# A Mamba block with adaptive layer norm on one core: chunk products by row halves, one PSUM tile for each burst of them, one ring of six PSUM banks, and a reordered front part

## The chip, the cores and the metric

The kernel runs on one core of one Trainium2 chip. The metric is the device time of one execution in microseconds (us); lower is better. The kernel before takes 829.81 us, the median of three runs (829.78, 829.81 and 830.87 us). One further execution was recorded by the hardware profiler.

The engines are named as in the profile. PE is TensorE, and its weight loads are listed apart as PEld. DVE is VectorE, ACT is ScalarE, POOL is GpSimd, and SP issues the DMAs (SPq is its queue). PSUM is the memory that PE writes its results into; a "bank" is the unit in which the kernel's PSUM pool hands it out.

## The reference, cut to what matters

All data are float32. There are 4 sequences of 512 tokens with 512 features. A modulation vector is computed for each sequence, then comes a Mamba layer, and then a square feed-forward layer whose weights are reduced to signs times a row mean:

```python
mod = (silu(c) @ wmod).reshape(4, 6, 1, 512)          # sa, ca, ga, sb, cb, gb
h = layernorm(x) * (1 + ca) + sa
x = x + ga * mamba(h)                                 # ga, gb: kept away from 0 by 0.25
h = layernorm(x) * (1 + cb) + sb
x = x + gb * (h @ binarize(W).T + bias)

# mamba(h), with d_inner 1024, 8 groups of state 64, 64 heads of size 16, chunks of 128 tokens
x, B, C, z, A = split(h @ in_proj.T)                  # 1024, 512, 512, 1024, 64
x, B, C = silu(causal_conv4([x, B, C]) + bias)
dt = softplus(A);  A_cum = cumsum(-dt) inside a chunk
Y_diag = sum over s' <= s of  (C_s . B_s') * exp(A_cum_s - A_cum_s') * x_s'
state  = state * exp(sum of -dt in the chunk) + sum over s of  B_s * exp(A_cum_end - A_cum_s) * x_s
Y_off  = (C_s . state before the chunk) * exp(A_cum_s)
y = Y_diag + Y_off + D * x / dt
out = (y * silu(z + z_bias)) @ out_proj.T
```

The change touches the two products with C: the scores `C . B` inside a chunk and `C . state` across chunks. Both contract over the 64 state entries of one group.

## The kernel before, in words

**Tiling.** The 2048 tokens are cut into eight halves `h` of 256 tokens (two for each sequence), each half into two chunks `c` of 128. The eight groups are taken in four pairs `gp`, so that one pair fills 128 partitions: 64 state entries of group r = 0, then 64 of r = 1. A unit is one `(h, c, gp)`, and there are 64 units. Features lie on partitions during the projections and the convolution.

**Front part of a half.** `f_norm` and `f_hT` normalize and transpose the tokens. `f_dt` (L296) makes softplus, the cumulative sums `pc`, the totals `pe`, turned copies `pn` and `pr`, and stores sums, exponentials and reciprocals to DRAM (L347, L350, L362). `conv_pair` (L369) projects two tiles of 128 channels on PE (four accumulating products each, L367), scales on ACT (L379), adds three convolution taps on DVE straight from PSUM (L383), and ends with a tanh on ACT and a product on DVE (L391). It is called for B, C and x. For C the last product is written twice, into the two diagonal blocks of a tile `cd` that is zero elsewhere (three such tiles, cleared once, L112 to L116). `to_tokens` (L394) transposes B and x back to tokens-on-partitions through PSUM. `f_xt` (L424) also loads the reciprocals from DRAM (`rr`, one buffer) and multiplies on POOL (L442), which is the last use of the tile `u` of that convolution (tag "u", two buffers). `f_z` (L445) makes the gate.

**Units.** `stage0` loads the cumulative sums, spread over partitions, into two of four `decay` tiles, and the factors `e` (L480 to L493). `stage1` (L500) forms the scores `pg` for both groups in one product: stationary 128x128 from B, moving 128x256 from the zero-padded `cd` (L509). DVE masks them (L511), ACT takes 16 exponentials (L516), DVE multiplies (L519). `stage2` (L524) forms `C . state` in the same way into half of the tile `py` (L543, left out for the first chunk of a sequence), then the products with x: sixteen of 32 output columns each for the two groups, four of them side by side in the array (L549). DVE and POOL combine (L557 to L562), and the new state is made on PE (`pst`, L574, 64 output columns each).

**Tail of a chunk.** `tail1` to `tail3` (L601 to L638) do the output projection `po`, the second layer norm, and the feed-forward `pf`.

**PSUM.** Four banks with the tag "mm" (projections, `phT`, `po`, `ph`, `pf`), two with "tr" (transposes, the small products of `f_dt`, `pst`), one for `pg`, one for `py`.

**Order.** `FRONT` gives each front function a step relative to its half; `at` collects functions by step, and the loop at L676 issues them step by step, with one unit per step: `stage1` of the next unit, the functions of the step, `stage2` of this unit, `stage0` of the unit after next. That is the order of priority. [...]

Of the kernel before, what the change touches and what calls it, by code (L numbers as in the profile page):

```python
# [1 line left out]

# [13 lines left out]
P = 128  # L16
# [5 lines left out]
KS = 4  # L22
# [16 lines left out]
def adaln_mamba_block(  # L39
# [28 lines left out]
    ps = ctx.enter_context(tc.tile_pool(name="ps", bufs=4, space=PSUM))  # L68
# [42 lines left out]

    cds = []  # L112
    for i in range(3):
        cd = keep.tile([P, 2, 2, T], F32, name=f"cd{i}")
        nc.gpsimd.memset(cd, 0.0)
        cds.append(cd)  # L116
# [66 lines left out]
    def mod_cols(t6, slot):  # L183

        pg = mod_row(t6)
        row = wk.tile([B, DM], F32, tag="h2", name=f"row{t6}")
        nc.vector.tensor_scalar(row, pg, 1.0 if t6 in (1, 4) else 0.0, None, ALU.add)
        pm = ps.tile([P, NK, B], F32, tag="tr", bufs=2, name=f"pm{t6}")
        for dt in range(NK):
            nc.tensor.transpose(pm[:, dt, :], row[:, dt * P : (dt + 1) * P], ident[:B, :B])  # L190
        nc.vector.tensor_copy(modT[:, slot], pm)
# [12 lines left out]
    def gates_out():  # L204

        grow = wk.tile([B, 3, DM], F32, tag="gates", name="grow", bufs=1)
        brow = wk.tile([B, DM], F32, tag="th", name="brow", bufs=1)
# [88 lines left out]
    def f_dt(h):  # L296
# [6 lines left out]
        pa = ps.tile([P, W], F32, tag="tr", bufs=2, name=f"pa_{h}")  # L303
# [4 lines left out]
        u, r, s, q, acc, relu = (small(n) for n in ("du", "dr", "ds", "dq", "da", "dl"))  # L308
# [5 lines left out]
        nc.vector.tensor_mul(s, u, r)  # L314
        nc.vector.tensor_mul(q, s, s)
        nc.vector.tensor_scalar(acc, q, SERIES[0], None, ALU.mult)
        for cf in SERIES[1:]:
            nc.vector.scalar_tensor_tensor(acc, acc, cf, q, ALU.add, ALU.mult)
        nc.vector.scalar_tensor_tensor(acc, acc, 1.0, s, ALU.add, ALU.mult)
        nc.vector.scalar_tensor_tensor(acc, acc, 2.0, relu, ALU.mult, ALU.add)  # L320
        ndt = small("ndt", 2)
        nc.vector.tensor_scalar(ndt, acc, -1.0, None, ALU.mult)
        drdt = small("drdt")
        nc.vector.reciprocal(r, acc)
        nc.vector.tensor_mul(
            drdt.rearrange("p (c h) -> p c h", c=2), r.rearrange("p (c h) -> p c h", c=2), bc_mid(dsk, 2)
        )

        pe = ps.tile([P, 2, W], F32, tag="tr", bufs=2, name=f"pe_{h}")
# [12 lines left out]
        pc = ps.tile([NH, 2, 2, CH], F32, tag="tr", bufs=2, name=f"pc_{h}")  # L342
# [8 lines left out]
        pn = ps.tile([P, W], F32, tag="tr", bufs=2, name=f"pn_{h}")  # L351
        for c in range(2):
            nc.tensor.transpose(pn[:, c * NH : (c + 1) * NH], sh[:, c, :], ident[:NH, :NH])
        st = small("st", 2)
        nc.vector.tensor_scalar(st, pn, -1.0, None, ALU.mult)

        pr = ps.tile([NH, 2, CH], F32, tag="tr", bufs=2, name=f"pr_{h}")
# [5 lines left out]
        H[h].update(ed=ed, dec=dec, st=st)  # L363

    def proj(pm, h, col, lo):
        for k in range(NK):
            mm(pm, win[:, k, col : col + P], H[h]["hT"][:, k, lo:], start=(k == 0), stop=(k == NK - 1))  # L367

    def conv_pair(h, t0, name, dst=None):  # L369
# [4 lines left out]
        u = wk.tile([P, 2, T], F32, tag="u", name=f"u_{name}_{h}", bufs=2)  # L374
        for j in range(2):
            t = t0 + j
            pm = ps.tile([P, KS - 1 + T], F32, tag="mm", name=f"pp_{name}{j}_{h}")
            proj(pm, h, t * P, 0)
# [7 lines left out]
        th = wk.tile([P, 2, T], F32, tag="th", name=f"th_{name}_{h}", bufs=1)  # L386
        nc.scalar.activation(th, u, AF.Tanh)
        if dst is None:
            dst = [(u, slice(0, P))]
        for d, r in dst:  # L390
            nc.vector.scalar_tensor_tensor(d, th[r], 1.0, u[r], ALU.add, ALU.mult)  # L391
        return u

    def to_tokens(src, name):  # L394

        pt = ps.tile([P, 2, 2, P], F32, tag="tr", bufs=2, name=f"pt_{name}")
# [5 lines left out]
    def f_B(h, q):  # L402
        t = wk.tile([P, 2, T], F32, tag="B", name=f"B_{h}_{q}", bufs=3)
        conv_pair(h, DI // P + 2 * q, f"B{q}", [(t, slice(0, P))])
        H[h]["B"][q] = t

    def f_C(h, q):
        cd = cds[(2 * h + q) % 3]
        conv_pair(
            h, (DI + NG * NS) // P + 2 * q, f"C{q}",  # L410
            [(cd[r * NS : (r + 1) * NS, :, r, :], slice(r * NS, (r + 1) * NS)) for r in range(2)],
        )
        H[h]["C"][q] = cd
# [7 lines left out]
    def f_x(h, j):  # L421
        H[h]["xc"] = conv_pair(h, 2 * j, f"x{j}")

    def f_xt(h, j):  # L424
        xc = H[h].pop("xc")
# [8 lines left out]
        rr = wk.tile([P, 2, T], F32, tag="rr", name=f"rr_{h}_{j}", bufs=1)  # L434
# [10 lines left out]
    def f_z(h, j):  # L445
        pm = ps.tile([P, 2, T], F32, tag="mm", name=f"pp_z{j}_{h}")
        for q in range(2):
            proj(pm[:, q, :], h, NCONV + (2 * j + q) * P, KS - 1)
        u = wk.tile([P, 2, T], F32, tag="u", name=f"uz_{h}_{j}", bufs=2)
# [4 lines left out]
        th = wk.tile([P, 2, T], F32, tag="th", name=f"thz_{h}_{j}", bufs=1)  # L454
# [9 lines left out]
    U0, U1 = {}, {}  # L464
# [32 lines left out]
    def c_pair(h, c, gp):  # L497
        return H[h]["C"][gp // 2][:, gp % 2, :, c * CH : (c + 1) * CH]

    def stage1(h, c, gp):  # L500
# [7 lines left out]
        pg = ps.tile([P, 2, CH], F32, tag="g", name=f"pg_{n}", bufs=1)  # L508
        mm(pg, H[h]["B"][gp // 2][:, gp % 2, c * CH : (c + 1) * CH], c_pair(h, c, gp), start=True, stop=True)  # L509
        gm = wk.tile([P, 2, CH], F32, tag="gm", name=f"gm_{n}", bufs=3)  # L510
        nc.vector.tensor_mul(gm, pg, bc_mid(upto, 2))  # L511
# [12 lines left out]
    def stage2(h, c, gp):  # L524
# [16 lines left out]
        py = ps.tile([P, 2, 2, CH], F32, tag="y", name=f"py_{n}", bufs=1)  # L541
        if k > 0:
            mm(py[:, 1], states[b, k][:, gp, :], c_pair(h, c, gp), start=True, stop=True)  # L543

        for r in range(2):
            for q in range(2):
                for j in range(HPG // 2):
                    i = 2 * j + q
                    mm(py[32 * j : 32 * j + 32, 0, r, :], xp[:, r * 2 * P + 32 * i : r * 2 * P + 32 * i + 32],  # L549
                       ets[r][:, i, :], start=(q == 0), stop=(q == 1))  # L550
# [5 lines left out]
        if k > 0:  # L556
            nc.vector.tensor_mul(t, py[:, 1], e)  # L557
            nc.vector.tensor_add(t, py[:, 0], t)  # L558
            nc.gpsimd.tensor_add(t, t, xs)  # L559
        else:  # L560
            nc.vector.tensor_add(t, py[:, 0], xs)  # L561
        nc.gpsimd.tensor_mul(zg, t, zg)  # L562

        if k < HPB * 2 - 1:
# [6 lines left out]
            pst = ps.tile([P, P], F32, tag="tr", bufs=2, name=f"pst_{n}")  # L571
# [57 lines left out]
    def tail3(h, c):  # L629
# [9 lines left out]


    FRONT = [
        (1, load_x, ()), (2, f_norm, ()), (3, f_hT, ()), (3, f_dt, ()),
        (4, f_B, (0,)), (4, f_C, (0,)), (4, f_Bt, (0,)),
# [90 lines left out]
```

## Time and profile before

| | before |
|---|---|
| median of three runs | 829.81 us |
| profiled execution, its own time | 828.1 us |
| its span, first to last instruction | 826.4 us |
| granted TensorE clock, mean of the span | 0.98 |
| PE busy | 773.7 us, 94% |
| DVE busy | 647.4 us, 78% |
| ACT busy | 529.2 us, 64% |
| POOL busy | 258.2 us, 31% |
| DMA moved | 99.26 MB, 120 GB/s in the mean |

A float32 product shows in the profile as two MATMUL rows, so 64 products `pg` appear as x128. The time that the profile gives for one MATMUL runs to its modelled end; the pace of PE is read from one row's start to the next row's start. A form such as `128*64 128x128` reads: 128 rows and 64 columns of the array are used, and the moving operand is 128 partitions by 128 elements. In the list of groups, the numbers behind the bar are the busy time as a union, the mean duration of one, and the idle time of that engine just before.

### The profile page before, as it was taken

What the parts mean: (1) busy time and instruction counts of PE and PEld (TensorE: products, weight loads), DVE (VectorE), ACT (ScalarE), POOL (GpSimd) and SP (SyncE); (2) the same over time, 40 slices, a digit from 0 to 9 for tenths busy, and PEclk for the clock granted to TensorE, in tenths of its full rate; (3) what the DMA queues carried; (4) which work ended last, traced back from release to release, by engine and by line L of the source; (5) the groups of instructions that cost most, each with busy time, mean ns of one, the idle gap of its engine ahead of it and who ended that gap; (6) DMA issues with size and microseconds to landing.
All of it is one profiled execution on the core that took longest, in us unless ns stands there. A gap on an engine that the chain in (4) does not pass through costs nothing. (4 is left out here: it accounts for less than half of the span.)

```text
span 826.4 us, 14794 instructions
## 1 busy us (share of the span) xinstructions
PE 773.7 (94%) x5008; PEld 531.7 (64%) x5008; DVE 647.4 (78%) x1249; ACT 529.2 (64%) x1510; POOL 258.2 (31%) x293
## 2 busy tenths in 40 slices
PE   5979889999999999999999999999999999999875
PEld 0853657767667767667667767667667766667431
DVE  3688779995899669995899669996899768995742
ACT  0455485677667778577767678476758687676640
POOL 5020312353223412353223412253213521353431
PEclk9979999999999999999999999999999999999986
DMA  8856542525344372425444272344434382343620
GB/s 297 324 136 199 148 103 68 136 62 137 94 116 127 87 180 68 129 70 128 103 112 133 74 190 68 104 94 104 128 101 113 91 204 52 113 103 90 147 58 13
DMA packets 120139, 99.26 MB, mean 120 GB/s; under 512 B 73976, under 2 KB 98552, under 8 KB 120064
## 3 DMA queue, kind: packets, MB, share of 16 engines
q1 hardware_dynamic: 120064, 98.32, 44.9%
q8 instruction: 40, 0.66, 0.4%
q14 instruction: 35, 0.29, 0.1%
HBM read 92.50 MB, written 5.79 MB: 119 GB/s over the span
## 5 line engine op out<-in xcount | busy, mean ns | idle before, releaser
L516 ACT ACTIVATE decay<-decay,st 128x128 f32<-128x128 f32 x1024 | 313.8, 390 | 39.5 <-DMA decay<-sums_d 39.0
L519 DVE SCALAR_TENSOR_TENSOR decay<-decay,gm 128x1024 f32<-128x1024 f32 x128 | 168.4, 1322 | 11.4 <-ACT decay L516 10.6
L367 PE MATMUL pp_x<-hT,win 128*128 128x259 f32 x512 | 124.5, 393 | 3.4 <-DVE u_B L383 3.4
L606 PE MATMUL po<-wout,z 128*128 128x512 f32 x256 | 122.0, 615 | 5.3 <-POOL z L562 5.3
L367 PE MATMUL pp_z<-hT,win 128*128 128x256 f32 x512 | 115.1, 379 | 0.0
L367 PEld LDWEIGHTS pp_x<-hT,win 128*128 128x128 f32 x512 | 95.6, 193 | 23.0 <-issue 7.7
L367 PEld LDWEIGHTS pp_z<-hT,win 128*128 128x128 f32 x512 | 95.4, 189 | 15.7 <-issue 3.3
L549 PE MATMUL py<-decay,xpad 128*32 128x128 f32 x2048 | 81.8, 280 | 6.6 <-DVE decay L519 5.4
L383 DVE SCALAR_TENSOR_TENSOR u_x<-pp_x,cw,u_x 128x256 f32<-128x256 f32 x192 | 81.8, 476 | 2.2 <-ACT u_x L379 1.7
L442 POOL TENSOR_TENSOR xs<-u_x,rr 128x512 f32<-128x512 f32 x32 | 47.2, 1474 | 112.7 <-DVE u_x L391 68.1
L606 PEld LDWEIGHTS po<-wout,z 128*128 128x128 f32 x256 | 47.2, 194 | 51.6 <-issue 44.1
L549 PEld LDWEIGHTS py<-decay,xpad 128*32 128x32 f32 x2048 | 54.1, 111 | 36.0 <-issue 23.8
L569 POOL TENSOR_TENSOR xd<-xpad,ed 128x256 f32<-128x256 f32 x48 | 35.2, 732 | 131.4 <-PE pst L574 101.8
L562 POOL TENSOR_TENSOR z<-yt,z 128x256 f32<-128x256 f32 x64 | 66.7, 1042 | 30.4 <-DVE yt L561 18.9
L559 POOL TENSOR_TENSOR yt<-yt,xs 128x256 f32<-128x256 f32 x48 | 38.9, 811 | 111.1 <-DVE yt L558 110.9
L634 PE MATMUL pf<-bwT,h 128*128 128x512 f32 x128 | 63.5, 636 | 6.6 <-DVE u_x L383 5.8
L367 PE MATMUL pp_B<-hT,win 128*128 128x259 f32 x256 | 60.6, 382 | 0.0
L367 PE MATMUL pp_C<-hT,win 128*128 128x259 f32 x256 | 58.9, 381 | 0.0
L623 ACT ACTIVATE h<-ph,modT 128x128 f32<-128x128 f32 x64 | 24.5, 456 | 48.7 <-PE ph L621 48.7
L451 ACT ACTIVATE uz<-pp_z,zb 128x256 f32<-128x256 f32 x64 | 26.9, 466 | 43.7 <-PE pp_z L367 41.7
L367 PEld LDWEIGHTS pp_B<-hT,win 128*128 128x128 f32 x256 | 47.5, 190 | 11.2 <-issue 4.3
L367 PEld LDWEIGHTS pp_C<-hT,win 128*128 128x128 f32 x256 | 48.4, 190 | 7.4
(129 smaller groups left out, 1083.3 us busy)
## 6 DMA issues: line engine op xcount, KB each, us to landing
decay<-sums_d SPq DMA_DIRECT2D x128, 256.0 KB
decay<-sums_d SPq DMA_DIRECT2D x128, 128.0 KB
rr<-r_d SPq DMA_DIRECT2D x64, 128.0 KB
wm<-in_w_mod SPq DMA_DIRECT2D x24, 256.0 KB
e<-e_d SPq DMA_DIRECT2D x96, 64.0 KB
x<-in_x SPq DMA_DIRECT2D x16, 256.0 KB
win<-in_w_inT SPq DMA_DIRECT2D x4, 1024.0 KB
xr<-in_x SPq DMA_DIRECT2D x16, 256.0 KB
```

The lines of the kernel that those rows point to most:

```text
L367: mm(pm, win[:, k, col : col + P], H[h]["hT"][:, k, lo:], start=(k == 0), stop=(k == NK - 1))
L383: nc.vector.scalar_tensor_tensor(u[:, j, :], pm[:, k : k + T], cw[:, t, k : k + 1], u[:, j, :], ALU.mult, ALU.add)
L442: nc.gpsimd.tensor_tensor(xs, xc, rr, ALU.mult)
L451: nc.scalar.activation(u[:, q, :], pm[:, q, :], AF.Identity, bias=zb[:, 2 * j + q : 2 * j + q + 1], scale=0.5)
L516: nc.scalar.activation(ets[r][:, i, :], ets[r][:, i, :], AF.Exp, bias=H[h]["st"][:, hd : hd + 1])
L519: nc.vector.scalar_tensor_tensor(ets[r], ets[r], 1.0, bc_mid(gm[:, r, :], HPG), ALU.min, ALU.mult)
L549: mm(py[32 * j : 32 * j + 32, 0, r, :], xp[:, r * 2 * P + 32 * i : r * 2 * P + 32 * i + 32], ets[r][:, i, :], start=(q == 0), stop=(q == 1))
L559: nc.gpsimd.tensor_add(t, t, xs)
L562: nc.gpsimd.tensor_mul(zg, t, zg)
L569: nc.gpsimd.tensor_tensor(xd, xg, by_head(H[h]["ed"][:, hd0 : hd0 + HPP]), ALU.mult)
L606: mm(po, H[h]["z"][g // 2][:, g % 2, c * CH : (c + 1) * CH], wout[:, g, :], start=(g == 0), stop=(g == NKI - 1))
L634: mm(pf, h2[:, k, :], bwT[:, k, :], start=(k == 0), stop=(k == NK - 1))
```

## The change

In the words of the code:

- C is kept as one ordinary tile (tag "C", three buffers) with one closing product in `conv_pair`; the three zero-padded tiles are gone.
- Each product with C becomes two, one for each half of the partitions (64 rows of the array, 128 moving elements). The two halves write different halves of a new PSUM tile `gy`, 4 KB for each partition, one buffer. `burst(old, new)` makes the products with the state of unit `old` and the scores of unit `new`, two units ahead, into the same tile.
- `glued` puts every product of a burst, and every one of the eight products of a group's `py`, behind the first of them and at a priority 1000 places higher, so that they stand together in PE's queue.
- All other PSUM tiles, `py` among them, share the tag "mm" with six buffers.
- `f_dt` is cut into `f_dt`, `f_sums` and `f_turned_sums`. These two, `f_Bt` and `f_xt` are called through `behind`, which puts their PE instructions behind the last projection traced so far for that half, and `FRONT` places them one projection later than before.
- Buffers: "u" from two to four, "th" and "rr" from one to two, `ndt` from two to one; the tiles `ds` and `drdt` reuse `du` and `dr`.
- The tail functions of a step come behind the front functions of later halves. `stage0` and `stage1` of the unit two ahead follow `stage2` directly.

```diff
-    ps = ctx.enter_context(tc.tile_pool(name="ps", bufs=4, space=PSUM))
+    ps = ctx.enter_context(tc.tile_pool(name="ps", bufs=6, space=PSUM))
...
-    cds = []
-    for i in range(3):
-        cd = keep.tile([P, 2, 2, T], F32, name=f"cd{i}")
-        nc.gpsimd.memset(cd, 0.0)
-        cds.append(cd)
...
-        ndt = small("ndt", 2)
+        ndt = small("ndt")
...
+    def f_sums(h):
...
+    def f_turned_sums(h):
...
     def proj(pm, h, col, lo):
         for k in range(NK):
-            mm(pm, win[:, k, col : col + P], H[h]["hT"][:, k, lo:], start=(k == 0), stop=(k == NK - 1))
+            last = mm(pm, win[:, k, col : col + P], H[h]["hT"][:, k, lo:], start=(k == 0), stop=(k == NK - 1))
+        return last.ins
...
-        u = wk.tile([P, 2, T], F32, tag="u", name=f"u_{name}_{h}", bufs=2)
+        u = wk.tile([P, 2, T], F32, tag="u", name=f"u_{name}_{h}", bufs=4)
...
-        if dst is None:
-            dst = [(u, slice(0, P))]
-        for d, r in dst:
-            nc.vector.scalar_tensor_tensor(d, th[r], 1.0, u[r], ALU.add, ALU.mult)
+        nc.vector.scalar_tensor_tensor(u if dst is None else dst, th, 1.0, u, ALU.add, ALU.mult)
...
-        pt = ps.tile([P, 2, 2, P], F32, tag="tr", bufs=2, name=f"pt_{name}")
+        pt = ps.tile([P, 2, 2, P], F32, tag="mm", name=f"pt_{name}")
...
-        rr = wk.tile([P, 2, T], F32, tag="rr", name=f"rr_{h}_{j}", bufs=1)
+        rr = wk.tile([P, 2, T], F32, tag="rr", name=f"rr_{h}_{j}")
...
+    def glued(products):
+
+        first = products[0]()
+        with tc.issue_after(first.ins), tc.high_priority(offset=1000):
+            for product in products[1:]:
+                product()
+
+    def by_rows(gy, slot, h, c, gp, stationary):
+
+        return [
+            partial(
+                mm, gy[:, r, slot, :], stationary[part],
+                H[h]["C"][gp // 2][part, gp % 2, c * CH : (c + 1) * CH], start=True, stop=True,
+            )
+            for r, part in enumerate((slice(0, NS), slice(NS, P)))
+        ]
+
+    def burst(old, new):
+
+        gy = ps.tile([P, 2, 4, CH], F32, tag="gy", bufs=1, name="gy_" + "_".join(map(str, old or new)))
+        products = []
+        if old is not None:
+            h, c, gp = old
+            k = (h % HPB) * 2 + c
+            if k > 0:
+                products += by_rows(gy, 1, h, c, gp, states[h // HPB, k][:, gp, :])
+                G[old, 1] = gy
+        if new is not None:
+            h, c, gp = new
+            products += by_rows(gy, 0, h, c, gp, H[h]["B"][gp // 2][:, gp % 2, c * CH : (c + 1) * CH])
+            G[new, 0] = gy
+        glued(products)
...
-        pg = ps.tile([P, 2, CH], F32, tag="g", name=f"pg_{n}", bufs=1)
-        mm(pg, H[h]["B"][gp // 2][:, gp % 2, c * CH : (c + 1) * CH], c_pair(h, c, gp), start=True, stop=True)
...
-        py = ps.tile([P, 2, 2, CH], F32, tag="y", name=f"py_{n}", bufs=1)
-        if k > 0:
-            mm(py[:, 1], states[b, k][:, gp, :], c_pair(h, c, gp), start=True, stop=True)
+        py = ps.tile([P, 2, CH], F32, tag="mm", name=f"py_{n}")
...
+    def behind(h, f, *args):
+
+        with tc.issue_after(H[h]["last"]):
+            f(h, *args)
...
-        (4, f_B, (0,)), (4, f_C, (0,)), (4, f_Bt, (0,)),
-        (5, f_x, (0,)), (5, f_xt, (0,)), (5, f_x, (1,)), (6, f_xt, (1,)),
-        (6, f_B, (1,)), (6, f_C, (1,)), (6, f_Bt, (1,)),
-        (7, f_x, (2,)), (7, f_xt, (2,)), (7, f_x, (3,)), (8, f_xt, (3,)), (8, f_z, (0,)),
+        (4, f_B, (0,)), (4, f_C, (0,)), (5, f_x, (0,)), (5, behind, (f_sums,)), (5, behind, (f_Bt, 0)),
+        (5, f_x, (1,)), (5, behind, (f_turned_sums,)), (5, behind, (f_xt, 0)),
+        (6, f_B, (1,)), (6, f_C, (1,)), (6, behind, (f_xt, 1)),
+        (7, f_x, (2,)), (7, behind, (f_Bt, 1)), (7, f_x, (3,)), (7, behind, (f_xt, 2)),
+        (8, f_z, (0,)), (8, behind, (f_xt, 3)),
...
+        new = units[step + 2 : step + 3] if step >= 0 else units[0:2]
         if step < 0:
-            stage0(*units[0])
-        if 0 <= step < len(units):
+            for unit in new:
+                burst(None, unit)
+                stage0(*unit)
+                stage1(*unit)
+        elif step < len(units):
+            if new or not is_first(*units[step][:2]):
+                burst(units[step], new[0] if new else None)
             stage2(*units[step])
-        if ahead and late:
-            stage1(*units[step + 1])
-        if step + 2 < len(units):
-            stage0(*units[step + 2])
+            for unit in new:
+                stage0(*unit)
+                stage1(*unit)
```

## The prediction

> **What bounds the kernel now.** I read the page's busy lines and slices first, then the stretches by time, then the PE timeline, the waits, and last the groups.
>
> ```profile
> PE 773.7 (94%) x5008; PEld 531.7 (64%) x5008; DVE 647.4 (78%) x1249; ACT 529.2 (64%) x1510; POOL 258.2 (31%) x293
> PE   5979889999999999999999999999999999999875
> PEclk9979999999999999999999999999999999999986
> 192.00:284.00 92.00, 91.44 (x613) 65.17 (x612) 78.08 (x149) 65.43 (x188) 28.73 (x30) 1.00 0.45 111
> 284.00:376.00 92.00, 88.85 (x611) 62.67 (x610) 76.42 (x149) 64.20 (x184) 30.78 (x36) 1.00 0.44 107
> ```
>
> From 100 to 780 us PE is busy nearly throughout (91.4 and 88.9 of 92 us, one half each) at the full granted clock; DVE follows with 76 to 78 of 92. So what counts is PE time in each unit, and after that PE's few gaps. The timeline of PE for one stretch shows the units:
>
> ```profile
> 454.23 0.60 PE L509 MATMUL pg<-cd,B 128*128 128x256 f32 x2
> 454.66 3.60 PE L606 MATMUL po<-wout,z 128*128 128x512 f32 x8
> 458.09 0.60 PE L399 MATMUL pt_xt<-ident,u_x 128*128 128x128 f32 x4
> 458.53 7.08 PE L367 MATMUL pp_z<-hT,win 128*128 128x256 f32 x32
> 465.53 1.08 PE L549 MATMUL py<-decay,xpad 128*32 128x128 f32 x32
> 466.55 0.44 PE L574 MATMUL pst<-xd,bt 128*64 128x128 f32 x4
> 466.91 0.70 PE L509 MATMUL pg<-cd,B 128*128 128x256 f32 x2
> 467.45 0.60 PE L621 MATMUL ph<-ident,t 128*128 128x128 f32 x4
> ```
>
> Start to start, a `pg` among full-array products costs 454.66 - 454.23 = 0.43 us, and right behind `pst` 467.45 - 466.91 = 0.54. So the first product after a change of array shape pays some 0.10 more (its second weight load isn't covered). The change of shape itself: 32 `pp_z` rows at their pace of 0.216 are 6.91, but 7.00 passed until `py` started: 0.09 a change. Four 128-element transposes take 0.44, 0.11 a pass. `pst`, four passes in two column halves, takes 0.36 with the 0.09 on leaving, so 0.27: its halves run side by side.
>
> PE's waits, and two that stand behind them:
>
> ```profile
> PE pf L634 <- DVE u_x L383: 5.8, 3, 1.9
> PE pe L330 <- DVE ndt L322: 3.9, 4, 1.2
> PE pp_x L367 <- DVE u_B L383: 3.4, 2, 2.9
> PE pt_bt L399 <- DVE B L391: 1.8, 4, 0.7
> PE py L543 <- DVE yt L558: 1.2, 1, 1.2
> ACT u_B L379 <- POOL xs L442: 2.4, 1, 2.4
> POOL xs L442 <- DMA rr<-r_d: 38.7, 11, 11.7
> ```
>
> Some 58 us of PE gaps in the whole span (start-to-start beyond the pace above, slow clock after a gap included) lie at the start, at the end and in these places.
>
> **The change part by part.** Its own time is 828.1 us with a span of 826.4; the median is 829.8, so 1.7 us over the profiled execution, which I add at the end.
>
> *Products by row halves.* 64 `pg` and 48 `C . state` products, 112 in all, cost 0.43 each. Each becomes two products of 64 rows and 128 elements, four passes. No row of this profile runs two row halves at once. Run in turn, four passes cost 0.44 (the transposes' row): no gain. Run side by side, like `pst`, two rounds of 0.11: 0.22. I take 0.22, since `pst` is the nearest row: two halves of the array, the same number of passes and elements, different outputs. 112 x 0.21 = 23.5 us less; the other end is 0, and an extra cost is kept in the next term.
>
> That weight loads of different tiles can run together shows in this row of the groups:
>
> ```profile
> L549 PEld LDWEIGHTS py<-decay,xpad 128*32 128x32 f32 x2048 | 54.1, 111 | 36.0 <-issue 23.8 <-DVE decay L519 6.9 <-ACT decay L516 2.9
> ```
>
> 2048 loads of 111 ns are 227 us, done in 54.1. [...]
>
> *Shape changes.* There will be 66 bursts: two at the start, 62 with a new unit, two at the end with an old one alone. Each is a shape of its own. In front of `py` it adds one change (0.09) and its own uncovered second load (0.10): 66 x 0.197 = 13.0 more. The 0.10 that `pg` pays now is paid by the full-array product that follows. If other work always stands between burst and `py`, it is 0.197 more each, 26 in all. Glueing goes the other way: the PE timeline has 103 runs of `py` rows for 64 units (at 413.3 to 416.1 one unit's is cut into four by `pn`, `pr` and `pst`); I expect 80, so 23 x 2 x 0.093 = 4.3 less (0 to 7). Net +8.7, bounds +6 and +26.
>
> *Gaps.* Near 50 to 62 us PE sits 2.6 us before `py`, then 2.9 before `pp_x`, and runs some 2.3 us slower after that. There ACT waits for a `u` tile that POOL holds until `rr` has landed. Four `u` and two `rr` lift that; late next is DVE's convolution, so I count 5. `behind` puts a projection (3.5 us, 16 passes) ahead of `pe` and `pt_bt`, which takes their 3.9 + 1.8. For `pf <- u_x` (5.8, and 1.8 of slow clock at 520) a bank of "mm" is held by the taps; six banks against four help, but `py`, `pst` and transposes now compete for them: half, 3.8. Together 14.5; gaps here come back elsewhere, since DVE is at 84% in these stretches and its chains aren't shorter. I take 7 less; bounds 15 less and, if the shared ring is the tighter one (six "mm" with `py` among them against four, two and one before), 5 more.
>
> *DVE, ACT, POOL.* The two closing products of C (32 of 905 ns, 29.0 us busy) become 16 like the x ones (842 ns), 13.5: 15.5 us less on DVE, hidden under PE, worth 0; without that cover up to 15 less. The cleared `cd` tiles (2.7 us of POOL) lay beside the first weight loads: 0. Reused small tiles: no instruction fewer; `ndt` with one buffer must be read by `pe` and `pc` before the next half's, a half later: 0.
>
> *Queues.* `f_sums` moves its two stores on SP (0.64 and 0.55 at 413.5) behind the projections of B, C and x0, and `f_turned_sums` moves the store of `r_d` (0.87) behind x1's. Queued behind them on SP are the `decay`, `e` and `rr` loads; ACT's exponentials and POOL's `xs` wait for those. SP itself mostly waits (258 us for `py` to free a `decay` tile), and the next half's first unit is three steps away: 0 in the middle. At the start the sums are due at 37.9 us, with x's projections done at the same time: 0, at most 3.5 more. Tails behind fronts in a step only change what fills in: 0. `burst` ahead of `py` makes the next burst wait for the DVE readers of `gy`; the row of that kind is `py <- yt L558`, 1.2 us: 0, and a rival.
>
> Sum: -23.5 + 8.7 - 7 = -21.8. Profiled: 806.3; median 808.
>
> **The rivals.** *Row halves run in turn.* For it: nothing here shows rows side by side. Against: columns do, four at a time. Then 0 + 8.7 - 7 = +1.7: 831.5, between 824 and 840 with the other bounds.
>
> *The burst waits (slower).* `gy` has one buffer, so PE at a burst waits until DVE has read the previous one (mask and `yt`), and with old and new glued, for the later of two readers. If that leaves PE idle 0.6 us at each of 66 bursts, it adds 39.6: 848. It decides from 21.8 / 66 = 0.33 us. For it: at 454.2 the scores were ready and DVE masked them only at 457.1, 2.3 us after their end. Against: `pg` and `py` have one bank each now, and PE lost 1.2 us to that; projections fill in.
>
> *More than forecast.* Bursts always next to `py`, every gap named gone, some of the tail's too: -23.5 + 6 - 15 = -32.5, 797; with DVE's cover relieved as well, 788.
>
> **How the numbers follow.** Forecast (800 to 818): 0.48. More: 0.17. In turn: 0.18, of it 0.05 faster, 0.04 the same, 0.09 slower. Burst waits: 0.17, of it 0.02 faster, 0.15 slower. A difference of 0.2% (1.7 us) is about what the runs can tell, which spread by 1.1 us. Faster 0.48 + 0.17 + 0.05 + 0.02 = 0.72, same 0.04, slower 0.24. The range leaves out the worst of the waiting rival and the best of the gains: 788 to 838; the forecast's own is 800 to 818.
>
> **What would show it.** Right: the pace of a four-product burst near 0.54 (0.22 + 0.22 + 0.10) and not 0.9; about as many shape changes as before plus 40; `pe`, `pt_bt` and the start's `u_B` gone from PE's waits; the DVE busy time near 632. Wrong: first-pass rows of a burst 0.11 apart for r = 0 and 1 (in turn); a new wait of PE on the mask or `yt` at the head of the waits; idle PE beside a busy DVE in the middle; or a start longer than 100 us to the first unbroken stretch.

## The result and the profile after

The changed kernel takes 855.93 us (median of four runs, 847.62 to 858.37). The kernel before, run beside it on the same chip, takes 830.34 us (829.78 to 831.22). The ratio is 1.029 with a 95% interval of 1.022 to 1.036: slower, where 808.0 was forecast, and beyond the upper end of the range, 838. The profiled execution takes 855.14 us; its span is 853.4 us against 826.4 before. Runs of one kernel differ by up to 15 us here, with the clock that they are granted (0.960 in the fastest of the changed kernel's four, 0.945 in the slowest), so differences of a few us between two kernels say little.

The page's busy lines and slices of the changed kernel:

```profile
PE 775.4 (91%) x5232; PEld 537.0 (63%) x5232; DVE 613.4 (72%) x1233; ACT 521.3 (61%) x1510; POOL 240.2 (28%) x290
PE   4898799899989999999989999899989999999875
PEclk9999999999899999999999979999999989999967
```

PE is busy 91% of the span, not 94%, and there are 8s in the middle of its line where before had an unbroken row of 9s. The same two stretches as in the prediction (start and end, length, then busy time of PE, PEld, DVE, ACT and POOL, granted clock, DMA share, GB/s):

```profile
192.00:284.00 92.00, 87.47 (x630) 63.87 (x629) 70.58 (x143) 59.30 (x173) 25.91 (x29) 0.94 0.43 112
284.00:376.00 92.00, 87.35 (x628) 62.15 (x627) 71.64 (x144) 62.53 (x182) 28.80 (x37) 0.98 0.42 110
```

PE is idle 4.5 and 4.7 us in them, where it was idle 0.6 and 3.2 before. So no other engine became the bound: DVE's busy time fell too, from 78.1 and 76.4 us to 70.6 and 71.6. PE loses time to waits, and these are its waits (total us, times, longest):

```profile
PE pt_xt L401 <- DVE u_x L393: 23.8, 14, 3.4
PE pg L175 <- DMA wm<-in_w_mod: 10.9, 2, 7.9
PE py L498 <- DVE decay L546: 7.1, 5, 2.5
PE pa L301 <- ACT hT L285: 5.0, 6, 1.2
...
PE gy L498 <- DVE gm L538: 4.5, 3, 1.5
...
PE gy L498 <- DVE yt L585: 0.4, 1, 0.4
```

The first line is new. PE stands before the transposes of x until DVE has finished the convolution, 14 times. `pe <- ndt`, `pt_bt <- B` and `pp_x <- u_B`, which the change was to remove, are gone, and so is `pf <- u_x`. One of the 14 places in PE's timeline, with what stands around it (start, busy us, instructions, and in brackets the idle time before and its releaser):

```profile
433.04 0.66 PE L401 MATMUL pt_bt<-ident,B 128*128 128x128 f32 x4
433.54 3.67 PE L371 MATMUL pp_x<-hT,win 128*128 128x259 f32 x16
...
437.69 0.28 PE L357 MATMUL pn<-ident,sh 64*128 64x64 f32 x2
437.90 0.41 PE L363 MATMUL pr<-ident,dr 128*64 128x128 f32 x2
440.55 0.66 PE L401 MATMUL pt_xt<-ident,u_x 128*128 128x128 f32 x4 [2.24 <-DVE u_x L393]
441.04 0.60 PE L649 MATMUL ph<-ident,t 128*128 128x128 f32 x4
441.57 0.40 PE L498 MATMUL py<-decay,xpad 128*32 128x128 f32 x1
...
443.43 3.90 PE L371 MATMUL pp_B<-hT,win 128*128 128x259 f32 x13
```

`pp_B` at 443.43 needs `hT`, which `pp_x` had already used at 433.54, and a bank; that of `pt_bt` had been read out by ACT at 435.84. By these it could have filled the 2.24 us, but it ran behind `pt_xt`. It also shows a second loss behind this gap: 13 rows in 3.90 us are 0.30 each, where the pace is 0.216. The granted clock in short stretches from 438 to 447 us (PE busy, granted clock, DMA share, GB/s) goes with it:

```profile
438.00:441.00 3.00, 0.76 (x6) 1.00 0.18 43
441.00:443.00 2.00, 2.00 (x34) 0.66 0.00 1
443.00:445.00 2.00, 2.00 (x16) 0.50 0.45 144
445.00:447.00 2.00, 2.00 (x11) 0.99 0.67 200
```

**Where the 28.6 us between PE's first and last row went.** For each pair of PE rows I took the time from start to start beyond the pace of the row's own shape, and summed what exceeds 0.16 us. That is "gaps", slow clock included; the rest of the time from PE's first row to its last is "products and shapes". The gaps are split in two: time in which PE is idle (first to last row less the page's busy time), and busy time beyond products and shapes, for the most part, as I read it, rows stretched by a lower clock (the clock's record has 32.9 us of the span at half before and 84.1 in the changed kernel). Each row of the table is from one profiled execution; experiments 1 and 5 are below.

| | PE, first to last row | products and shapes | gaps | of them idle | of them stretched |
|---|---|---|---|---|---|
| before | 811.9 | 753.5 | 58.4 | 38.2 | 20.2 |
| changed | 840.5 | 737.1 | 103.4 | 65.1 | 38.3 |
| experiment 1 | 817.4 | 736.8 | 80.6 | 42.3 | 38.3 |
| experiment 5 | 805.4 | 735.7 | 69.7 | 45.1 | 24.6 |

So the part that the change was meant to save is saved, 16.4 us, and 45.0 us of new gaps cost more than that: 26.9 us of idle time and 18.1 us of stretched rows (the granted clock is 0.951 in the mean of the span, 0.980 before).

**The reason, by the order of PE's rows.** The order is that of the rows' start times. In the changed kernel 438 tiles take a buffer from the shared ring "mm", and their first writers run exactly in the order in which the program text asks for the tiles: none of the 438 is out of it. In the kernel before, of the 364 tiles in "mm" and "tr" (ten of the opening left out) none is out of order inside its own ring (224 and 140 tiles), but 97 are out of order across the two. So in these two profiles first writers left program order only from one ring to the other, never inside one. In the one ring no projection ran ahead of a transpose that the program asked for earlier, though the transpose still waited for DVE (23.8 us in 14 waits). The prediction's "projections fill in" was seen here only across rings.

### The profile page after: what moved, and what is told of

The parts are those of the page before. It is cut to its first block, busy times and chain, and to the rows that moved or that the text cites. A ratio compares the mean times of both kernels' runs of the same rounds, so it can differ in the third digit from the quotient of the medians.

```text
span 853.4 us, 15226 instructions
## 1 busy us (share of the span) xinstructions
PE 775.4 (91%) x5232; PEld 537.0 (63%) x5232; DVE 613.4 (72%) x1233; ACT 521.3 (61%) x1510; POOL 240.2 (28%) x290
## 4 chain that ended last, share of the span: by engine, by line
PE 71%; ACT 13%; DVE 8%; DMA 3%; issue 3%; POOL 1%; SPq 1%; DVEq 0%; ACTq 0%; POOLq 0%
PE po L634 12%; PE pp_z L371 12%; ACT decay L543 9%; PE pp_B L371 7%; PE pp_x L371 7%; PE pp_C L371 6%; PE pf L662 6%; PE py L501 4%; PE py L498 4%; DVE decay L546 3%; PE pa L301 3%; PE pt_xt L401 2%; PE pg L175 2%; PE pst L602 2%; PE gy L498 2%
## 5 line engine op out<-in xcount | busy, mean ns | idle before, releaser
L371 PE MATMUL pp_x<-hT,win 128*128 128x259 f32 x512 | 118.9, 384 | 0.0
L634 PE MATMUL po<-wout,z 128*128 128x512 f32 x256 | 114.8, 600 | 0.1
L587 POOL TENSOR_TENSOR yt<-yt,xs 128x256 f32<-128x256 f32 x48 | 42.4, 884 | 154.5 <-DVE yt L586 144.3
L501 PE MATMUL py<-decay,xpad 128*32 128x128 f32 x1792 | 79.3, 297 | 0.0
L371 PE MATMUL pp_B<-hT,win 128*128 128x259 f32 x256 | 70.8, 430 | 0.0
L384 ACT ACTIVATE u_x<-pp_x,cb,cw 128x256 f32<-128x256 f32 x64 | 35.0, 560 | 55.9 <-PE pp_x L371 55.9
L498 PE MATMUL py<-decay,xpad 128*32 128x128 f32 x256 | 55.1, 300 | 7.3 <-DVE decay L546 7.1
L371 PEld LDWEIGHTS pp_B<-hT,win 128*128 128x128 f32 x256 | 53.1, 216 | 12.8 <-issue 2.9
L441 POOL TENSOR_TENSOR xs<-u_x,rr 128x512 f32<-128x512 f32 x32 | 43.4, 1355 | 59.7 <-DMA rr<-r_d 35.0
L590 POOL TENSOR_TENSOR z<-yt,z 128x256 f32<-128x256 f32 x64 | 54.9, 857 | 15.6 <-DVE yt L589 11.9
L388 DVE SCALAR_TENSOR_TENSOR u_B<-pp_B,cw,u_B 128x256 f32<-128x256 f32 x96 | 45.1, 471 | 18.0 <-ACT u_B L384 16.8
```

The source lines that it names most:

```text
L371: last = mm(pm, win[:, k, col : col + P], H[h]["hT"][:, k, lo:], start=(k == 0), stop=(k == NK - 1))
L384: nc.scalar.activation(u[:, j, :], pm[:, KS - 1 :], AF.Identity, bias=cb[:, t : t + 1], scale=cw[:, t, KS - 1 : KS])
L388: nc.vector.scalar_tensor_tensor(u[:, j, :], pm[:, k : k + T], cw[:, t, k : k + 1], u[:, j, :], ALU.mult, ALU.add)
L441: nc.gpsimd.tensor_tensor(xs, xc, rr, ALU.mult)
L498: first = products[0]()
L501: product()
```

## The experiments

All times are medians, all ratios are against the kernel before on the same chip. "After" in an edit means the changed kernel.

**1. Two rings again.** After, with the shared ring cut in two: four banks for projections, `phT`, `po`, `ph` and `pf`; two for the transposes and small products, with `py` and `pst` among them.

```diff
-    ps = ctx.enter_context(tc.tile_pool(name="ps", bufs=6, space=PSUM))
+    ps = ctx.enter_context(tc.tile_pool(name="ps", bufs=4, space=PSUM))
...
-        pt = ps.tile([P, 2, 2, P], F32, tag="mm", name=f"pt_{name}")
+        pt = ps.tile([P, 2, 2, P], F32, tag="tr", bufs=2, name=f"pt_{name}")
...
-        py = ps.tile([P, 2, CH], F32, tag="mm", name=f"py_{n}")
+        py = ps.tile([P, 2, CH], F32, tag="tr", bufs=2, name=f"py_{n}")
```

(and the same for `pm`, `pa`, `pe`, `pc`, `pn`, `pr`, `pst`)

> The kernel after, with its six shared PSUM buffers split again: four with the tag mm for projections and tails, two with tr for transposes, the small products of the front part, pst and py. Nothing else is changed. Theory O (order): in one ring the buffers are handed out in the order of the program, so no projection can be placed ahead of an earlier transpose or py that still waits, and PE stands idle; two rings let projections pass. O expects 815 to 838 us, with the wait of pt_xt for u_x down from 23.8 us to under 12. Theory C (capacity): six buffers are too few with py among them; a split of the same six is tighter, so C expects 856 or more. Theory F (front): the new places of the sums and turned tiles are what is late; F expects 848 to 860, unchanged.

Measured: 828.04 us (820.61 to 833.52), ratio 0.989 (0.984 to 0.995). The same banks in two rings are 28 us faster than in one by the medians (23 us between the two profiled executions). Lines of its list of PE's waits:

```profile
PE py L498 <- DVE decay L546: 3.5, 3, 1.9
...
PE pt_xt L401 <- DVE u_x L393: 1.5, 5, 0.5
```

The wait of `pt_xt` falls from 23.8 to 1.5 us, and the timeline shows the same place of the program with projections let through:

```profile
427.16 0.41 PE L363 MATMUL pr<-ident,dr 128*64 128x128 f32 x2
427.40 1.92 PE L371 MATMUL pp_B<-hT,win 128*128 128x259 f32 x8
429.41 0.63 PE L401 MATMUL pt_xt<-ident,u_x 128*128 128x128 f32 x4
429.87 1.11 PE L371 MATMUL pp_B<-hT,win 128*128 128x259 f32 x4
430.91 0.30 PE L498 MATMUL py<-decay,xpad 128*32 128x128 f32 x1
```

Eight rows of `pp_B` run between `pr` and `pt_xt`, and PE doesn't wait. Of the same 364 first writers 56 are again out of program order across the rings. Gaps are 80.6 us instead of 103.4, and all of the difference is idle time; products and shapes, 736.8 us, and the stretched rows stay as they were.

**2. The same single ring, one bank shorter.** After, `bufs=6` made `bufs=5`.

```diff
-    ps = ctx.enter_context(tc.tile_pool(name="ps", bufs=6, space=PSUM))
+    ps = ctx.enter_context(tc.tile_pool(name="ps", bufs=5, space=PSUM))
```

> The kernel after with five buffers in the shared ring in place of six. O: the order of PE's work is set by the single ring, not by its length, so 850 to 865 us and the same waits. C: one buffer less of a resource that runs out must cost visibly more, 870 us or above, with PE waits that a free buffer ends (DVE taps, ACT copies) at the head of the list. F: unchanged, 848 to 862.

Measured: 859.9 us, ratio 1.026 (1.017 to 1.035), the same as the changed kernel; `pt_xt <- u_x` is 22.7 us in 15 waits. Banks aren't short in the one ring: a sixth less moves nothing that these runs can tell, so it is the single order that costs, not the number of buffers.

**3. One ring in the kernel before.** Before, with "mm" and "tr" made one ring of the same six banks. Nothing else of the change is in it.

```diff
-    ps = ctx.enter_context(tc.tile_pool(name="ps", bufs=4, space=PSUM))
+    ps = ctx.enter_context(tc.tile_pool(name="ps", bufs=6, space=PSUM))
...
-        pt = ps.tile([P, 2, 2, P], F32, tag="tr", bufs=2, name=f"pt_{name}")
+        pt = ps.tile([P, 2, 2, P], F32, tag="mm", name=f"pt_{name}")
```

(and the same for `pm`, `pa`, `pe`, `pc`, `pn`, `pr`, `pst`)

> The kernel before with one edit: its four mm and two tr buffers become one ring of six; pg and py keep their own banks, and the row halves, the new front order and the larger buffers are all left out. O: it slows down like the kernel after, to 845 to 875 us, with PE waits on DVE and ACT results that were filled before and a lower granted clock. C: the same number of buffers, more freely shared, so 822 to 832. F: the front order is the old one, so 826 to 832.

Measured: 1010.16 us, ratio 1.215 (1.210 to 1.220). The direction is that of the ring order, the size far above what was expected. The head of its list of PE's waits:

```profile
PE py L549 <- DVE decay L519: 38.8, 23, 3.8
PE pt_xt L399 <- DVE u_x L391: 30.6, 16, 3.3
PE pg L509 <- DVE gm L511: 16.8, 8, 3.3
PE py L543 <- DVE yt L558: 15.3, 10, 2.6
PE pt_bt L399 <- DVE B L391: 14.9, 12, 2.1
```

None of the 364 first writers is out of program order now, and gaps are 238 us instead of 58. In the old order of the front part a transpose follows its own projection directly, and in the one ring no later projection ran ahead of it. The changed kernel's calls through `behind` put a projection between. That is a likely reason why the same ring costs it 28 us and not 180; it was not tried apart.

**4. The tails in their old place.** Experiment 1, with the tail functions of a step called ahead of the front functions of later halves again, as before.

```diff
-    for h in range(NHALF):
         for c in range(2):
             end = h * NU + (c + 1) * NP
```

> As e1, and the tail functions of a step stand ahead of the front functions again, as before the change. If the tails' later place takes filler from PE where hT and the softplus chain are late (pa waits for hT, 5.0 us in the kernel after), this is 4 to 10 us below e1. If the ring alone is the cause, it is within 3 us of e1.

Measured: 830.78 us, ratio 1.000 (0.998 to 1.002), against 0.989 (0.984 to 0.995) for experiment 1: slower, but by what amount the spread of experiment 1 leaves open. Experiment 11 settles it.

**5. Cover ahead of `pa`.** What stays in experiment 1 is a wait directly behind the turned tokens `phT` in the seven later halves. In three of them `pa`, the first product of `f_dt`, waits 1.2 us, in one 3.1 us for the load of x, and in three `gy` waits 1.5 us for DVE's mask:

```profile
PE gy L498 <- DVE gm L538: 4.5, 3, 1.5
PE pa L301 <- DVE yt L586: 3.5, 3, 1.2
...
PE pa L301 <- DMA x<-in_x: 3.1, 1, 3.1
```

The lower clock isn't where the edit looked for it. Behind the 1.2 us of `pa` (at 211 us) the granted clock stays at 1.00, and behind the other two of that kind. Behind the 1.5 us of `gy` (at 301 us) it falls to half, as it does behind the other two waits of `gy` and behind the 3.1 us (the 92 us from 192, 376 and 560 have 1.00 in the mean, those from 100, 284, 468 and 652 have 0.91, 0.96, 0.94 and 0.94):

```profile
211.00:213.00 2.00, 2.00 (x26) 1.00 0.82 235
...
303.00:305.00 2.00, 2.00 (x17) 0.50 0.45 114
```

Here the last gate projection of the previous half is called between `f_hT` and `f_dt`.

```diff
+    def f_z_before(h):
+        if h > 0:
+            f_z(h - 1, NP - 1)
+
...
-        (1, load_x, ()), (2, f_norm, ()), (3, f_hT, ()), (3, f_dt, ()),
+        (1, load_x, ()), (2, f_norm, ()), (3, f_hT, ()), (3, f_z_before, ()), (3, f_dt, ()),
...
-        for j in range(1, NP):
+        for j in range(1, NP if h == NHALF - 1 else NP - 1):
```

> As e1 (rings of four and two), and the last gate projection f_z of the half before is called between f_hT and f_dt, so that 3.5 us of PE work stands between the turned tokens phT and pa. If what is left of e1's loss is the gap of 1.3 to 1.7 us before pa once in each half and the slow clock behind it (half rate for some 4 us), the time falls by 10 to 25 us against e1, to 803 to 818, with the granted clock up from 0.954 to 0.97 or above. If the slow clock has other sources, less than 4 us.

Measured: 819.22 us (815.78 to 820.02), ratio 0.984 (0.981 to 0.988). This is the fastest version (with 9 and 10, which can't be told from it), faster than both kernels. The page of its profile:

```profile
PE 760.3 (93%) x5232; PEld 520.6 (64%) x5232; DVE 615.7 (75%) x1233; ACT 526.3 (64%) x1510; POOL 248.7 (30%) x290
PE   4999699999999999999999999999999999999775
```

The middle is again an unbroken row of 9s. `pa` is left with one wait of 0.9 us, in the first half, and `gy` waits 2.5 us for the mask, 0.8 at the longest. Gaps are 69.7 us instead of 80.6: PE is idle 2.8 us longer than in experiment 1, and the stretched rows are 13.7 us less (clock 0.972 in the mean, 0.954 there). So the gain is in the stretched rows. The waits behind which the clock was at half in experiment 1 are shorter or gone (three of `gy`, 4.5 us then and 2.5 now; the 3.1 us of `pa`); that they brought the lower clock is my reading, and no run shows how.

**6. Small buffers.** Experiment 1, with "u" back at two buffers and "th" at one.

```diff
-        u = wk.tile([P, 2, T], F32, tag="u", name=f"u_{name}_{h}", bufs=4)
+        u = wk.tile([P, 2, T], F32, tag="u", name=f"u_{name}_{h}", bufs=2)
...
-        th = wk.tile([P, 2, T], F32, tag="th", name=f"th_{name}_{h}")
+        th = wk.tile([P, 2, T], F32, tag="th", name=f"th_{name}_{h}", bufs=1)
```

(and the same where `f_z` and the opening take these tags)

> As e1 with the tag u back at two buffers and th at one (rr stays at two). The prediction gave the larger buffers some 5 us, at the start. If so, 830 to 836; if they matter in every half, 836 or more; if not at all, e1's 828 within 3 us. It is also the reference for e7.

Measured: 867.99 us, ratio 1.044 (1.041 to 1.047), 40 us above experiment 1. From PE's and from ACT's list of waits:

```profile
PE pf L662 <- DVE u_B L388: 17.7, 7, 4.2
```

```profile
ACT u_B L384 <- POOL xs L441: 28.9, 7, 6.5
```

ACT can't begin a convolution until POOL has read the `u` tile of an earlier one, so DVE's taps on the projections in PSUM come late, and `pf` waits for their bank. `f_xt`, which ends the use of `u`, is called one projection later than before, so the new order leans on the four buffers. In the kernel before, with two buffers and the old order, all of ACT's waits for `xs` were 5.8 us. What "th" has of the 40 us was not separated.

**7. Whole products.** Experiment 6, with the two row halves of a product joined into one of 128 rows on a zero-padded `cd`, as before, still in one burst and glued.

```diff
-                mm, gy[:, r, slot, :], stationary[part],
-                H[h]["C"][gp // 2][part, gp % 2, c * CH : (c + 1) * CH], start=True, stop=True,
+                mm, gy[:, slot], stationary,
+                H[h]["C"][gp // 2][:, gp % 2, :, c * CH : (c + 1) * CH], start=True, stop=True,
```

> As e6 with whole products in place of the row halves: the three zero-padded tiles of C are back (which is why the buffers are the small ones), each product has 128 rows and 256 elements, and gy has the same size and the same bursts. It prices the row halves. By the prediction's terms, products 23.5 us less and an added change of shape and an uncovered load for each burst 13.0 more, e7 is 10 us above e6; side by side without the added changes 23; if the gain is lost in waits, within 3 us.

Measured: 875.81 us, ratio 1.053 (1.045 to 1.061). The row halves are worth some 8 us by the medians, though the intervals of 6 and 7 overlap. The two profiled executions show products and shapes of 743.7 us against 738.2, 5.5 less with the halves. Experiment 7 also has C's two closing products on DVE again.

**8. The old order of the front part.** Experiment 1, with `FRONT` as before and the sums directly behind `f_dt`, and no `behind`.

```diff
-        (4, f_B, (0,)), (4, f_C, (0,)), (5, f_x, (0,)), (5, behind, (f_sums,)), (5, behind, (f_Bt, 0)),
-        (5, f_x, (1,)), (5, behind, (f_turned_sums,)), (5, behind, (f_xt, 0)),
...
+        (3, f_sums, ()), (3, f_turned_sums, ()),
+        (4, f_B, (0,)), (4, f_C, (0,)), (4, f_Bt, (0,)),
+        (5, f_x, (0,)), (5, f_xt, (0,)), (5, f_x, (1,)), (6, f_xt, (1,)),
```

> As e1 with the FRONT list of the kernel before: f_sums and f_turned_sums directly behind f_dt at step 3, f_Bt and f_xt directly behind their convolutions, and no issue_after on them. If the new front order helps once the rings are apart, e8 is 5 to 20 us above e1, with PE waits of pe for ndt and of pt_bt and pt_xt for their convolutions; if the order is what hurts, e8 is below e1; if neither, within 4 us.

Measured: 845.51 us, ratio 1.017 (1.013 to 1.021), 17 us above experiment 1. So the later turned tiles and sums are a gain even when the rings are apart. How they gain stays open: the waits that were expected here, `pe`, `pt_bt` and `pt_xt` for their convolutions, come to 1.8 us in its list, and longer waits of `ph`, `po`, `pf` and `pa` head it. Why this version is 14 us slower than the kernel before it ran beside (831.31 us), though it has the row halves, was not separated; `py` sharing the two banks of the transposes, the bursts two units ahead with one `gy`, and the tails' place are among what else differs.

**9. The halves in turn.** Experiment 5, with the four products of a burst issued as both of the upper half of the rows (old unit, new unit), then both of the lower half.

```diff
-        glued(products)
+        glued(products[0::2] + products[1::2])
```

> As e5, with the four products of a burst in another order: both of row half 0 first, then both of row half 1, where e5 alternates. Same products, same loads. If the halves gain because neighbours in the queue use different halves of the array, a burst of four takes about 0.75 to 0.95 us in place of 0.53 and the kernel 10 to 25 us more than e5, 829 to 844. If the array sorts them itself, within 3 us of e5.

Measured: 819.53 us, ratio 0.986 (0.981 to 0.990), the same as experiment 5. A burst in its timeline (S is the state, B the scores; L498 is the first product of a burst, L501 the others):

```profile
405.45 0.37 PE L498 MATMUL gy<-C,S 64*128 64x128 f32 x1
405.46 0.37 PE L501 MATMUL gy<-C,S 64*128 64x128 f32 x1
...
405.77 0.40 PE L501 MATMUL gy<-C,B 64*128 64x128 f32 x4
406.10 0.30 PE L498 MATMUL py<-decay,xpad 128*32 128x128 f32 x1
```

The lower half's product S started 0.01 us after the upper half's, although the program issues the upper half's product B between the two. The trace doesn't show the queue itself, but the edit did reach the chip: in all 46 bursts of four the two starts are 0.013 or 0.014 us apart, in experiment 5 0.006 or 0.007. So the order of issue couldn't be used to make the halves run one after the other.

**10. No glue.** Experiment 5, with the products of a burst and of `py` issued without the extra order and priority.

```diff
-        first = products[0]()
-        with tc.issue_after(first.ins), tc.high_priority(offset=1000):
-            for product in products[1:]:
-                product()
+        for product in products:
+            product()
```

> As e5 without glued: the products of a burst and of py are issued one by one at their own priority, with no issue_after. If the glue saves changes of array shape (the prediction gave it 4.3 us, 0 to 7), 819 to 827 with more runs of py rows than e5; if it costs because PE must wait for a whole group, 810 to 818; if the order comes out nearly the same, within 3 us.

Measured: 819.09 us, ratio 0.986 (0.982 to 0.989): no difference to experiment 5. In the profiled executions there are 364 shape changes instead of 351, since 66 bursts fall into 77 pieces, and products and shapes take 739.6 us instead of 735.7, but the gaps are 65.2 us instead of 69.7. What glue saves in shapes comes back in the gaps. The runs of `py` rows are 75 without the glue and 74 with it.

**11. Experiment 5 with the tails in their old place** (the edit of experiment 4).

```diff
-    for h in range(NHALF):
         for c in range(2):
             end = h * NU + (c + 1) * NP
```

> As e5 with the tail functions ahead of the front functions in a step, as in the kernel before. With the rings apart the tails can fill gaps from either place: within 4 us of e5, 815 to 823. If their later place is what lets pf wait for its ACT results (6.1 us in e5), 2 to 6 us below e5.

Measured: 827.13 us, ratio 0.995 (0.992 to 0.998), 8 us above experiment 5. Tails behind the fronts are a gain.

**12. Three rings.** Experiment 5, with three banks for "mm", two for the small ones, and one for `py` alone.

```diff
-    ps = ctx.enter_context(tc.tile_pool(name="ps", bufs=4, space=PSUM))
+    ps = ctx.enter_context(tc.tile_pool(name="ps", bufs=3, space=PSUM))
...
-        py = ps.tile([P, 2, CH], F32, tag="tr", bufs=2, name=f"py_{n}")
+        py = ps.tile([P, 2, CH], F32, tag="y", bufs=1, name=f"py_{n}")
```

> As e5 with the six shared PSUM buffers as three rings: three mm, two tr without py, one for py alone, as the kernel before had one bank for it. By theory O a py that no longer stands in the order of the transposes can start earlier, 812 to 819. If three projection banks are too few for DVE's taps, PE waits on DVE taps come to the head of the list and it is 822 to 835.

Measured: 829.9 us, ratio 0.999 (0.996 to 1.001), 11 us above experiment 5. The head of its list of PE's waits:

```profile
PE pp_C L371 <- DVE u_B L388: 11.9, 4, 3.2
```

A projection waits for a bank that DVE's taps still read. `py` on its own doesn't pay for a fourth projection bank.

## Why the prediction was wrong, by its own steps

**Products by row halves: right.** The burst of four at 387.61 in the changed kernel's timeline, up to `py`:

```profile
387.61 0.37 PE L498 MATMUL gy<-C,S 64*128 64x128 f32 x1
387.62 0.37 PE L501 MATMUL gy<-C,S 64*128 64x128 f32 x1
387.82 0.27 PE L498 MATMUL gy<-C,S 64*128 64x128 f32 x1
387.83 0.27 PE L501 MATMUL gy<-C,S 64*128 64x128 f32 x1
387.94 0.39 PE L501 MATMUL gy<-C,B 64*128 64x128 f32 x4
388.26 0.30 PE L498 MATMUL py<-decay,xpad 128*32 128x128 f32 x1
```

The two row halves start 0.01 us apart, and from the first row to `py` pass 0.65 us, of which 0.09 is the change of shape. The prediction said 0.54 and 0.09. The rival that the halves run in turn is out. The weight loads of the two halves overlap as well: in this burst the first two (at 387.61 and 387.62) take 0.18 us each, about as long as the 0.19 of a full-array load (`po` at 453.37 in the kernel before), and start 0.01 us apart.

**Shape changes: right in sum.** There are 333 against 310 before, 23 more where 40 were expected. Products and shapes together fell by 16.4 us; the two terms summed to 14.8. Experiments 6 and 7 put the row halves' own part near 8 us; the two terms give 23.5 - 13.0 = 10.5. The glue's 4.3 rested on fewer runs of `py` rows. They did fall, from 103 to 74, but by experiment 10 that isn't the glue's work; what the glue does is keep bursts whole, which is 4 us of products and shapes and nothing in the time.

**Gaps: the step that failed.** It had 7 us less, with bounds of 15 less and 5 more; 45 us more came. The single effects that it named did happen: the waits of `pe`, `pt_bt`, `u_B` and `pf <- u_x` went. What it got wrong is the clause "if the shared ring is the tighter one", which took the ring as a number of banks, six against four and two and one, and priced it at 5. In experiment 2 five banks in the one ring took 859.9 us where six took 855.9, which these runs can't tell apart. What counts is the order in the one ring: none of the 438 first writers ran out of program order, so the projections that covered the waits of transposes and of `py` ran ahead of them no more. Experiment 1 gives the price, 28 us; experiment 3, one ring alone in the kernel before, 180 us. Of the 45.0 us of new gaps two rings take away 22.8, all of it idle time. The sign that speaks against one ring was to be had from the kernel before: its timeline has projections placed around `pt_bt` and `pt_xt`, and these tiles had a tag of their own. The step also had no term for new stretches at a lower clock, which are 18.1 of the 45.0 us: the cover of experiment 5 takes away 13.7 of these and adds 2.8 of idle time. The last 11.3 us of the 45.0 stay open.

In the same step four `u` and two `rr` stood for 5 us, the end of one wait at the start. By experiment 6 the larger "u" and "th" are worth 40 in the new order, in which every later `f_xt` leans on `u`; that order and buffers depend on each other was not seen.

**DVE, ACT, POOL: right in price, short in size.** DVE's busy time fell by 34 us to 613.4, where 15.5 and about 632 were expected. Experiment 7, with C's two closing products again, has 627.0, experiment 6 has 612.1, so 14.9 of it came as expected; the rest has no explanation here. It bought nothing while PE was the bound.

**Queues: half right.** None of the moved stores or the loads behind them stands in PE's waits; the one DMA in the list, `wm`, belongs to the opening. But "tails behind fronts in a step only change what fills in: 0" is 8 us by experiment 11: what fills in is what sets PE's gaps here. The longer start was one of the signs given for a wrong forecast, and it came: PE is busy 75.8 of the first 100 us, 80.9 before, and 83.9 of the next 92, 88.0 before.

**The rival "the burst waits": real, but small.** Waits of `gy` for DVE's mask are 4.5 us in three places and 0.4 for `yt`. Behind two of the three the clock was at half for some 10 us, which is 5 lost each time, so they cost some 15 us in all, an estimate from these rows. The rival had 39.6, and would have decided from 0.33 us for each of the 66 bursts, 21.8 in all.

**The sums.** Two ends don't follow from the terms: "in turn" has 840 at its upper end, but 8.7 and 5 more give 843.5, and with 26 for the shapes 860.8; "more than forecast" has 788 with DVE's cover relieved, which takes 9 of a term of up to 15 without a reason. None of this changes the forecast.

The result lies outside all cases with a mechanism of their own, since none of them was about the order of the ring. With that part undone (experiment 1) the change gives 828.0, and with the cover behind `phT` 819.2. The forecast of 808 was not reached by any version. In the profiled execution of experiment 5 products and shapes are 735.7 us, 17.8 less than before, so what stands between it and the forecast is again gaps, 69.7 against 58.4.

## What to carry to other kernels

Before tiles of different kinds are put into one ring of buffers, ask which of them must be able to overtake which: where one ring held them all, in the changed kernel and in experiment 3, no first writer ran out of program order (0 of 438 and of 364), and with two rings 97 and 56 of 364 did, across the rings. By these runs, work that is to fill a wait belongs in another ring than the work that waits. Count a ring's orders, not only its banks; two rings of four and two beat one of six by 28 us with the same memory. An order that calls a consumer later needs the buffers it then holds longer, so the two are priced together.

## What the runs showed of the hardware

**Row halves of the array.** Two 64-row float32 products on the two halves of the rows ran side by side: in the burst at 387.61 of the changed kernel the starts are 0.01 us apart, and the rounds start at 387.61, 387.82, 387.94 and 388.05, so 0.21 us for the first and 0.11 for each after it. In the first round the second weight load starts 0.11 us in, at 387.72, and its product another 0.11 later, at 387.82. The issue order of experiment 9 made no difference in time (819.53 us against 819.22), and in its 46 bursts of four the lower half's product S started 0.013 or 0.014 us after the upper half's, although the program issues the upper half's product B between them. Whether PE's queue has the program's order there, the trace doesn't show.

**Half clock after short gaps.** In the changed kernel a wait of 2.24 us from 438.3 was followed by a granted clock of 0.66 and 0.50 until about 445. Another, 1.50 us before 501.6, was followed by 0.5 from 503 to 513 us:

```profile
501.60:503.00 1.40, 1.36 (x22) 1.00 0.94 238
503.00:505.00 2.00, 2.00 (x24) 0.52 0.61 155
...
511.00:513.00 2.00, 2.00 (x6) 0.50 1.12 259
513.00:515.00 2.00, 2.00 (x10) 0.92 0.15 48
```

In both PE was busy all the while. In the clock's record the half clock lasted 3.4 us behind the first and 10.2 us behind the second; why, isn't settled. From 503 to 513 us the DMA engines moved 155 to 339 GB/s. Idle times of 1.5 and 2.24 us were followed by it, but not each time: all six waits of 2.1 to 2.5 us before `pt_xt` from 250 us on were (3.4 us at half each), and two of the three of 1.5 us before `gy` (10.2 us each), while of three of 1.95 us before `pf` in the kernel before (at 334, 520 and 709) only that at 520 was (3.4 us). The first of the stretches above lost another 1.7 us by it (4 us at 0.58 in the mean), the second some 5 (10.2 us at half).
